# Output stage of a masked triangle product: x added by an accumulating gather for half of the columns, one bias addition on GpSimd

## The chip, the cores and the metric

One core of one Trainium2 chip. The metric is the device time of one execution in microseconds, the median of the runs shown. The engines are TensorE (PE in the profile, its weight loads PEld), VectorE (DVE), ScalarE (ACT), GpSimd (POOL) and SyncE (SP, which only issues transfers); 16 DMA engines move data between the chip's main memory (DRAM) and the on-chip SBUF. Each engine works through its own queue in order and waits on semaphores of the others.

## The reference, cut to what matters

x is 512 x 512 positions of 64 channels, float32. Two layers add to it:

```
x = x + conv0(groupnorm(x))      # layer 0
x = x + spectral(groupnorm(x))   # layer 1: 12 x 12 lowest Fourier modes, mixed over channels

conv0(g):
  n     = layernorm(g)
  left  = (n @ left_w  + left_b ) * mask * sigmoid(n @ lgate_w + lgate_b)
  right = (n @ right_w + right_b) * mask * sigmoid(n @ rgate_w + rgate_b)
  gate  = sigmoid(n @ ogate_w + ogate_b)
  u     = layernorm(einsum('bkjd,bkid->bijd', left, right)) @ out_w + out_b
  return u * gate
```

The part that matters here is the end of layer 0: x1 = x + u * sigmoid(rs * (x' @ W) + ogate_b), where rs is the reciprocal standard deviation of a position.

## The kernel before, in words

The mask has one value per row, and only rows with the mask set take part in the triangle product, so the kernel sorts those rows to the front (`src_i` holds for each rank the row of x) and computes the product for at most 256 rows. The `compact` branch is the one that runs. Its stages: statistics of x (to about 180 us), left and right factors, the triangle product, then the **output stage** that the change touches (first the layer norm and output weights of the product, giving u, then the units described below, about 800 to 1450 us), and a final stage that adds the Fourier part and writes the result (bound by its transfers).

In the output stage a **unit** is 32 columns j of two blocks of 128 rows: 128 partitions x 64 positions x 64 channels, two megabytes. There are 32 units (16 column groups by two halves of the ranks). The half with ranks from 256 on has no masked row: there u is only the row `bias_row_out`. A unit is worked in 8 steps n of 8 positions, and its 64 positions also make four tiles c = 0..3 of 16 positions, `z_t` (128 x 1024 elements, four buffers). Half r = 0 of a unit is c = 0 and 1, half r = 1 is c = 2 and 3.

The order of work is written out by hand: one loop over steps s issues, for every engine, the instructions of step s, and no scheduler moves them. v is the unit, n the step. In one step:

- TensorE: `transpose(s + 13)` (four 128 x 128 transposes of x, L1038; ScalarE copies them out, L1040), `times` with the gate weights into `w_ps` (L1045, two buffers), `times` with the centring matrix for step s + 12 into `c_ps` (L1045, two buffers), and at n = 0 and 4 of the next unit `transform` (L1140), the column Fourier sums of the finished halves r = 0 and r = 1.
- ScalarE: the copy L1040, the sigmoid of one tile at even n (L1221), at n = 5 the square root for the next unit (`root`, L1089, which loads another function table, as the sigmoid after it does again), the square of `c_ps` (L1076), and after every second unit the copy `save` (L1148).
- VectorE: four of the 32 group statistics of the unit before (`statistics`, L1168, from n = 3 on), every second step a reduction of the squares (L1083), the product of `w_ps` and rs (L1274), and at odd n the bias addition of the tile just completed (L1280). Every fourth unit it joins statistics (L1173 to L1186).
- GpSimd: `gated` (L1109), z = z * u, at odd n, and `added` (L1113), x = x + z, at even n, four of each per unit; and two gathers of x (L638, `load`, 1 MB each) for the unit v + 3 at n = 3 and n = 6. Both run on the GpSimd queue; a gather lands in one of five rotating x buffers (`places`).
- SyncE: `store` (L1129) writes a finished half of x1 to DRAM, r = 0 at n = 7 of its unit and r = 1 at n = 3 of the next; `load_u` (L1100) issues 32 small copies of u every second unit.

The order of GpSimd's queue in a unit before, from n = 3: gated(0), gather, added(0), gated(1), added(1), gather, gated(2), then in the next unit's steps 0 to 2 added(2), gated(3), added(3). The last tile of the last unit goes a way of its own (`finished`, on VectorE).

Of the kernel before, what the change touches and what calls it, by code (L numbers as in the profile page):

```python
# [17 lines left out]
P = 128  # L18
N = 512
C = 64  # L20
# [26 lines left out]
def conv_preact_kernel(ctx: ExitStack, tc: tile.TileContext, t: dict):  # L47
# [573 lines left out]
    def compact(fc):  # L621
# [12 lines left out]
            hb[:, :, :M2].rearrange("p b (m k) -> p b m k", k=2), slot_t[:, :, 2:].rearrange("p b (k m) -> p b m k", k=2)  # L634
        )

        def gather(dst, src, idx, r, jc):
            nc.gpsimd.indirect_dma_start(  # L638
                out=dst, out_offset=None, in_=src, in_offset=bass.IndirectOffsetOnAxis(ap=idx[:, r, jc : jc + 1], axis=0)
            )  # L640

        def slots_of(engine, jc, first=0, last=JC):
# [188 lines left out]
        with tc.tile_pool(name="tri", bufs=1) as trp:  # L831
# [92 lines left out]
            with tc.manual_schedule(), tc.tile_pool(name="late", bufs=1) as lp:  # L924
# [65 lines left out]
                with tc.tile_pool(name="np_x", bufs=LEAD + 2) as tp, tc.tile_pool(name="np_q", bufs=2) as sqp, tc.tile_pool(  # L990
# [28 lines left out]
                    def x_of(k):  # L1019
                        return place(order[k % RING])  # L1020
# [67 lines left out]
                        rss[k] = small.tile([P, SIZE * 8], F32, name="rs_n")  # L1088
                        nc.scalar.activation(rss[k], totals[k % 2], AF.Sqrt, bias=eps, scale=1.0 / C)  # L1089

                    def load(k, r):
                        jc, half = units[k]
                        gather(
                            x_of(k)[:, r * JC : (r + 1) * JC].rearrange("p j c -> p (j c)"), tiles, src_i, 2 * half + r, jc
                        )

                    def load_u(jc):
# [4 lines left out]
                    def gated(k, c):  # L1102

                        jc, half = units[k]
                        if half == 0:
                            u = us[jc][:, 16 * (c % 2) : 16 * (c % 2) + 16, c // 2, :]
                        else:
                            u = rows_of["out"].unsqueeze(1).to_broadcast([P, 16, C])
                        nc.gpsimd.tensor_mul(zs[k, c], zs[k, c], u)  # L1109

                    def added(k, c):
                        xr = x_of(k)[:, 16 * c : 16 * c + 16, :]
                        nc.gpsimd.tensor_add(xr, xr, zs.pop((k, c)))  # L1113
# [79 lines left out]
                    for s in range(-LEAD, total_g + 2 * SIZE):  # L1193
# [3 lines left out]
                        def held(i):  # L1197
                            return 0 <= v - i < len(units)
# [13 lines left out]
                            del xts[s]  # L1212
                        if 0 <= s + LEAD - 1 < total_g:
                            cps = centered(s + LEAD - 1)
                        if n in (0, 4) and held(1):
                            transform(v - 1, n // 4)

                        if n % 2 == 0:
                            i, c = (0, n // 2 - 1) if n >= 2 else (1, 3)
                            if held(i):  # L1220
                                nc.scalar.activation(zs[v - i, c], zs[v - i, c], AF.Sigmoid)  # L1221
                        if n == 5 and 0 <= k + 1 < first + len(units):
# [5 lines left out]
                        if n == 3 and held(2) and v % 4 == 1:  # L1228
                            join_squares(v // 4 - 1)

                        if n % 2 == 1:
                            i, c = (0, (n - 3) // 2) if n >= 3 else (1, 3)
                            if held(i) and (v - i, c) != (last, 3):
                                gated(v - i, c)
                            elif held(i):
                                finished()
                        else:
                            i, c = (0, (n - 4) // 2) if n >= 4 else (1, 2 + n // 2)
                            if held(i) and (v - i, c) != (last, 3):
                                added(v - i, c)  # L1240
                        if 0 <= v + 3 < len(units):
                            if n == 3:
                                load(v + 3, 0)
# [20 lines left out]
                        if wps is not None:  # L1264
                            c, odd = divmod(n, 2)
                            if not odd:
                                z = zp.tile([P, 16, C], F32, name="z_t")
                            if k < first:
                                rs = factors[k % 2][:, 16 * c : 16 * c + 16].rearrange("p (h e i) -> p h e i", h=2, e=2)
                                rs = rs[:, :, odd].unsqueeze(3).to_broadcast([P, 2, 4, C])  # L1270
                                nc.vector.tensor_mul(of_pair(z, odd), wps, rs)
                            else:
                                rs = rss[k][:, 8 * n : 8 * n + 8].unsqueeze(2).to_broadcast([P, 8, C])
                                nc.vector.tensor_mul(z[:, 8 * odd : 8 * odd + 8, :], wps, rs)  # L1274
                            if odd:
                                if k < first:
                                    bias = rows_of["out"].unsqueeze(1).to_broadcast([P, 16, C])
                                    nc.gpsimd.tensor_add(z, z, bias)  # L1278
                                else:
                                    nc.vector.tensor_add(z, z, bias_ps["ogate"].unsqueeze(1).to_broadcast([P, 16, C]))  # L1280
                                if k < first:
                                    j = JC * k + 8 * c
                                    nc.sync.dma_start(
                                        u_d[:, j : j + 8].rearrange("p j r c -> p (j r c)"), z.rearrange("p n c -> p (n c)")
                                    )
                                else:
                                    zs[v, c] = z

                        if n == 7 and held(0) and v < last:
                            store(v, 0)  # L1290
                        if n == 3 and held(1) and v - 1 < last:
                            store(v - 1, 1)
                        if n == 6 and v - 1 == last:
# [240 lines left out]
```

## Time and profile before

| | |
|---|---|
| runs shown | 1771.41, 1774.15, 1779.44 us; median 1774.15 |
| profiled execution | 1777.78 us, its span 1776.0 us |
| TensorE, VectorE, ScalarE, GpSimd busy over the span | 88%, 80%, 53%, 53% |
| DRAM read, written | 311.60 MB, 204.60 MB |
| 64 gathers of x in the output stage | GpSimd 983 ns each, landing 6.4 us after issue (median) |
| 127 sums and 127 products on GpSimd (L1113, L1109) | 2372 and 2371 ns each |
| 128 bias sums on VectorE (L1280) | 1221 ns each |
| 128 sigmoids on ScalarE (L1221) | 1058 ns each |

How to read the profile: the page gives busy times of the engines over the span and in 40 slices of 44.4 us. The windows table gives the same for stretches of one's choice. A line of the groups or of the timeline names start and duration in us, engine, code line, operation, out<-in by the program's names, shape, count, and in brackets how long the engine was idle ahead of it and which engine ended that. A DMA line gives the median time from issue to landing.

### The profile page before, as it was taken

How to read it: one execution, taken by the hardware profiler on the slowest of the kernel's cores; microseconds unless marked ns; L12 is line 12 of the kernel's file. 1: busy time of each engine (PE TensorE's matmuls, PEld its weight loads, DVE VectorE, ACT ScalarE, POOL GpSimd, SP SyncE). 2: the span in 40 equal slices, each digit the busy share in tenths (PEclk: the TensorE clock that was granted, in tenths of full speed). 3: DMA queues.
4: the chain of work that ended last, by engine and by line, in shares of the span. 5: the costliest groups of instructions: out<-in, count | busy, mean ns of one | idle time of the engine just before them, and what ended most of it. 6: DMA issues, size and time to landing. Idle time of an engine off the chain costs nothing. (4 is left out here: it accounts for less than half of the span.)

```text
span 1776.0 us, 32619 instructions
## 1 busy us (share of the span) xinstructions
PE 1567.8 (88%) x10918; PEld 1242.0 (70%) x10918; DVE 1413.7 (80%) x2982; ACT 933.0 (53%) x1660; POOL 936.5 (53%) x695
## 2 busy tenths in 40 slices
PE   6779799997999978899999999999999977998772
PEld 5667666662899867787888888888888745665341
DVE  7989678887455568688999999999999984865451
ACT  3666566663333266676777777777777742011000
POOL 4666211111000037698999999999999881111110
PEclk9999999999899999899999999999999976555555
DMA  7999278878898789868767767776776699999999
GB/s 281 386 386 388 107 206 227 229 229 245 279 305 303 257 246 347 298 196 296 265 242 257 253 233 259 264 249 239 249 264 244 212 318 400 425 427 427 426 427 385
DMA packets 192593, 518.48 MB, mean 292 GB/s; under 512 B 37664, under 2 KB 104480, under 8 KB 151456
## 3 DMA queue, kind: packets, MB, share of 16 engines
q1 hardware_dynamic: 156112, 295.65, 47.5%
q0 software_dynamic: 32832, 218.45, 33.4%
q10 hardware_dynamic: 3472, 2.20, 0.5%
q8 instruction: 89, 1.46, 0.3%
q14 instruction: 88, 0.72, 0.1%
HBM read 311.60 MB, written 204.60 MB: 291 GB/s over the span
## 5 line engine op out<-in xcount | busy, mean ns | idle before, releaser
L1045 PE MATMUL w_ps<-gate_x,xt_c 128*128 128x128 f32 x2048 | 280.5, 281 | 30.0 <-DVE z_t L1274 28.6
L1113 POOL TENSOR_TENSOR places<-places,z_t 128x1024 f32<-128x1024 f32 x127 | 301.3, 2372 | 8.0
L1045 PEld LDWEIGHTS w_ps<-gate_x,xt_c 128*128 128x128 f32 x2048 | 252.0, 194 | 46.4 <-DVE z_t L1274 44.6
L1045 PE MATMUL c_ps<-center_x,xt_c 128*128 128x128 f32 x2048 | 277.0, 279 | 0.8 <-ACT xt_c L1040 0.4
L1045 PEld LDWEIGHTS c_ps<-center_x,xt_c 128*128 128x128 f32 x2048 | 252.8, 194 | 3.8 <-ACT xt_c L1040 3.0
L1440 PE MATMUL l_ps<-places,rinv 24*128 24x512 f32 x512 | 206.2, 1118 | 29.3 <-DVE places L1447 19.0
L1168 DVE BATCH_NORM_STATS2 stats2c<-places 128x6 f32<-128x128 f32 x1024 | 220.5, 278 | 9.9 <-POOL places L1113 9.9
L1083 DVE TENSOR_REDUCE scratch<-sq_c 128x16 f32<-128x1024 f32 x160 | 194.6, 1216 | 31.1 <-ACT sq_c L1078 16.1
L1221 ACT ACTIVATE z_t<-z_t 128x1024 f32<-128x1024 f32 x128 | 135.5, 1058 | 131.8 <-DVE z_t L1280 131.1
L1440 PEld LDWEIGHTS l_ps<-places,rinv 24*128 24x128 f32 x512 | 119.8, 302 | 110.8 <-DVE places L1447 56.9
L1278 POOL TENSOR_TENSOR z_t<-z_t,bias_row_out 128x1024 f32<-128x1024 f32 x32 | 75.6, 2363 | 226.3 <-PE y_ps L1058 202.1
L1040 ACT ACTIVATE xt_c<-t_ps,ab_xc 128x512 f32<-128x512 f32 x256 | 176.0, 688 | 11.5 <-PE t_ps L1038 10.6
L1274 DVE TENSOR_TENSOR z_t<-w_ps,rs_n 128x512 f32<-128x512 f32 x256 | 172.0, 672 | 6.2 <-PE w_ps L1045 6.1
L1076 ACT ACTIVATE sq_c<-c_ps 128x512 f32<-128x512 f32 x256 | 150.8, 589 | 31.4 <-PE c_ps L1045 30.8
L1280 DVE TENSOR_TENSOR z_t<-z_t,scratch 128x1024 f32<-128x1024 f32 x128 | 156.3, 1221 | 9.9 <-ACT rs_n L1089 3.7
L688 DVE BATCH_NORM_STATS2 stats1c<-x_ps 128x6 f32<-128x512 f32 x256 | 157.1, 682 | 7.7 <-PE x_ps L687 7.4
L1109 POOL TENSOR_TENSOR z_t<-z_t,places 128x1024 f32<-128x1024 f32 x64 | 151.8, 2371 | 14.6 <-ACT z_t L1221 14.4
L1038 PE MATMUL t_ps<-c_ident,places 128*128 128x128 f32 x1024 | 158.4, 278 | 0.0
L1038 PEld LDWEIGHTS t_ps<-c_ident,places 128*128 128x128 f32 x1024 | 118.5, 142 | 51.4 <-issue 51.4
L1447 DVE TENSOR_TENSOR places<-places,l_ps 128x512 f32<-128x512 f32 x176 | 109.3, 682 | 55.2 <-DMA places<-x_h,dst_i 42.1
L1109 POOL TENSOR_TENSOR z_t<-z_t,bias_row_out 128x1024 f32<-128x1024 f32 x63 | 149.4, 2372 | 5.8 <-ACT z_t L1221 5.5
L673 ACT COPY xc<-xg 128x128 f32 x352 | 105.0, 298 | 66.1 <-POOL xc L673 47.1
(214 smaller groups left out, 2557.0 us busy)
## 6 DMA issues: line engine op xcount, KB each, us to landing
x_h<-places SPq DMA_DIRECT2D x64, 1024.0 KB
out_x<-places SPq DMA_DIRECT2D x44, 1024.0 KB
places<-u_d SPq DMA_DIRECT2D x512, 64.0 KB
out_x<-lx_t SPq DMA_DIRECT2D x20, 1024.0 KB
rbc<-rs_d POOLq DMA_DIRECT2D x32, 512.0 KB, 7.1
left_d<-o_c SPq DMA_DIRECT2D x64, 256.0 KB
right_d<-o_c SPq DMA_DIRECT2D x64, 256.0 KB
left_raw<-left_d SPq DMA_DIRECT2D x64, 256.0 KB
```

The source lines that it names most:

```text
L688: nc.vector.bn_stats(stats[:, 0, 16 * (jc % quarter) + 4 * r + c, :], ps.rearrange("p i k -> p (i k)"))
L1038: nc.tensor.transpose(tps[:, i, :], flat[:, o : o + P], ident)
L1040: nc.scalar.activation(xts[s], tps, AF.Identity, bias=ab1[:, 2:3])
L1045: nc.tensor.matmul(ps[:, 2 * i : 2 * i + 2, :], xts[s][:, i, :], w, start=True, stop=True)
L1076: nc.scalar.activation(sq, cps, AF.Square)
L1083: nc.vector.tensor_reduce(totals[k % 2][:, 8 * (n - 1) : 8 * (n + 1)], sqs.pop(s // 2), AX.X, ALU.add)
L1109: nc.gpsimd.tensor_mul(zs[k, c], zs[k, c], u)
L1113: nc.gpsimd.tensor_add(xr, xr, zs.pop((k, c)))
L1168: nc.vector.bn_stats(st[k // 4][:, g, k % 4, :], x_of(k)[:, :, 2 * g : 2 * g + 2])
L1274: nc.vector.tensor_mul(z[:, 8 * odd : 8 * odd + 8, :], wps, rs)
L1280: nc.vector.tensor_add(z, z, bias_ps["ogate"].unsqueeze(1).to_broadcast([P, 16, C]))
L1440: nc.tensor.matmul(ps.rearrange("p j o -> p (j o)"), rinv[h, b, :], it[h], start=True, stop=True, tile_position=(32 * g, 0),)
```

## The change

For tiles c = 0 and 1 (half r = 0 of a unit) `gated` writes the product over x in the x buffer, and x is added by a second gather of the same megabyte with the operation add, at n = 7; `added` is left for c = 2 and 3. The bias of tile c = 1 is added on GpSimd at n = 4 (`biased`, new), no longer on VectorE. With it, the sigmoids move from n = 0, 2, 4, 6 to 0, 2, 5, 6; the products from n = 1, 3, 5, 7 to 1, 3, 6, 7; the transform of half r = 0 from n = 0 to n = 2 of the next unit; its store from n = 7 to n = 1 of the next unit.

```diff
-        def gather(dst, src, idx, r, jc):
+        def gather(dst, src, idx, r, jc, op=ALU.bypass):
             nc.gpsimd.indirect_dma_start(
-                out=dst, out_offset=None, in_=src, in_offset=bass.IndirectOffsetOnAxis(ap=idx[:, r, jc : jc + 1], axis=0)
+                out=dst, out_offset=None, in_=src, in_offset=bass.IndirectOffsetOnAxis(ap=idx[:, r, jc : jc + 1], axis=0),
+                compute_op=op,
             )
...
-                        nc.gpsimd.tensor_mul(zs[k, c], zs[k, c], u)
+                        if c < 2:
+                            nc.gpsimd.tensor_mul(x_of(k)[:, 16 * c : 16 * c + 16, :], zs.pop((k, c)), u)
+                        else:
+                            nc.gpsimd.tensor_mul(zs[k, c], zs[k, c], u)
+
+                    def biased(k, c):
+                        bias = rows_of["ogate"].unsqueeze(1).to_broadcast([P, 16, C])
+                        nc.gpsimd.tensor_add(zs[k, c], zs[k, c], bias)
...
-                        if n in (0, 4) and held(1):
+                        if n in (2, 4) and held(1):
                             transform(v - 1, n // 4)
 
-                        if n % 2 == 0:
-                            i, c = (0, n // 2 - 1) if n >= 2 else (1, 3)
+                        if n in (0, 2, 5, 6):
+                            i, c = {0: (1, 3), 2: (0, 0), 5: (0, 1), 6: (0, 2)}[n]
                             if held(i):
                                 nc.scalar.activation(zs[v - i, c], zs[v - i, c], AF.Sigmoid)
...
-                        if n % 2 == 1:
-                            i, c = (0, (n - 3) // 2) if n >= 3 else (1, 3)
+                        if n == 7 and held(0):
+                            load(v, 0, ALU.add)
+                        if n in (1, 3, 6, 7):
+                            i, c = {1: (1, 3), 3: (0, 0), 6: (0, 1), 7: (0, 2)}[n]
                             if held(i) and (v - i, c) != (last, 3):
                                 gated(v - i, c)
                             elif held(i):
                                 finished()
-                        else:
-                            i, c = (0, (n - 4) // 2) if n >= 4 else (1, 2 + n // 2)
-                            if held(i) and (v - i, c) != (last, 3):
-                                added(v - i, c)
+                        if n == 4 and held(0):
+                            biased(v, 1)
+                        if n in (0, 2):
+                            c = 2 + n // 2
+                            if held(1) and (v - 1, c) != (last, 3):
+                                added(v - 1, c)
...
-                                else:
+                                elif c != 1:
                                     nc.vector.tensor_add(z, z, bias_ps["ogate"].unsqueeze(1).to_broadcast([P, 16, C]))
...
-                        if n == 7 and held(0) and v < last:
-                            store(v, 0)
+                        if n == 1 and held(1) and v - 1 < last:
+                            store(v - 1, 0)
```

More of the change, by code (lines that the diff above doesn't have):

```diff
@@ L1089, in root, with load @@
                         nc.scalar.activation(rss[k], totals[k % 2], AF.Sqrt, bias=eps, scale=1.0 / C)
-                    def load(k, r):
+                    def load(k, r, op=ALU.bypass):
                         jc, half = units[k]
                         gather(
-                            x_of(k)[:, r * JC : (r + 1) * JC].rearrange("p j c -> p (j c)"), tiles, src_i, 2 * half + r, jc
+                            x_of(k)[:, r * JC : (r + 1) * JC].rearrange("p j c -> p (j c)"), tiles, src_i, 2 * half + r, jc, op
                         )
```

## The prediction, as put on record

> **What bounds the kernel now.** I read the busy tenths by slice first (the output stage is slices 18 to 32, the only ones with PE, DVE and POOL all near 9), then the windows table inside that stage, then the timelines of one unit.
>
> ```profile
> core 0: us, PE busy (x) PEld busy (x) DVE busy (x) ACT busy (x) POOL busy (x), PEclk, DMA share, GB/s
> 860.00:940.00 80.00, 76.75 (x653) 67.92 (x652) 78.86 (x186) 58.89 (x89) 76.95 (x38) 1.00 0.71 254
> ```
>
> VectorE works 78.86 of 80 us, GpSimd 76.95, TensorE 76.75: three engines with almost no room, at a full clock. The DMA engines still have 29% free. GpSimd's timeline of one unit:
>
> ```profile
> 849.53 2.38 POOL L1113 TENSOR_TENSOR places<-places,z_t 128x1024 f32<-128x1024 f32 x1
> 851.85 2.38 POOL L1109 TENSOR_TENSOR z_t<-z_t,bias_row_out 128x1024 f32<-128x1024 f32 x1
> 854.31 2.36 POOL L1113 TENSOR_TENSOR places<-places,z_t 128x1024 f32<-128x1024 f32 x1
> 856.83 0.98 POOL L638 DMA_INDIRECT places<-in_x,src_i  x1
> 857.82 2.40 POOL L1109 TENSOR_TENSOR z_t<-z_t,bias_row_out 128x1024 f32<-128x1024 f32 x1
> ...
> 867.39 2.37 POOL L1109 TENSOR_TENSOR z_t<-z_t,places 128x1024 f32<-128x1024 f32 x1
> 869.90 0.98 POOL L638 DMA_INDIRECT places<-in_x,src_i  x1
> 870.91 2.38 POOL L1113 TENSOR_TENSOR places<-places,z_t 128x1024 f32<-128x1024 f32 x1
> ```
>
> No line carries an idle time: eight products and sums and two gathers fill the unit, 849.53 to 870.91 = 21.38. Start to start: a sum takes 2.32, a product 2.46, either before a gather 2.52, a gather 1.00. Over the stage the first gather of a unit starts at 805.87 and, 26 units later, at 1372.69: **21.80 us a unit**. Three in four take 21.3 to 21.4, set by GpSimd; every fourth 22.4 or more, when VectorE's join of the statistics makes GpSimd wait. So GpSimd binds, and VectorE (1.4% idle) is right behind.
>
> **The change, part by part**, per unit (32 units).
>
> VectorE loses one bias sum: 1.22 (L1280 mean 1221 ns). It then has about 20.3 of work in a unit.
>
> GpSimd loses two sums, gains a bias sum of the same shape (the nearest row, L1278 in the earlier stage, is 2363 ns, so 2.4) and a third gather. The order is now: bias(1), product(1), gather, adding gather, product(2), sum(2), product(3), sum(3), next unit's product(0), gather. Without waits: bias 2.37; product(1) 2.52; two gathers 2.00; 2.46 + 2.32 + 2.46 + 2.32 = 9.56; product(0) and gather 3.52. Sum 19.97, which would be a gain of 1.4.
>
> Two new waits eat it. **First gap:** between bias(1) and product(1) stands ScalarE's sigmoid of the same tile, and GpSimd has nothing queued between them. Sigmoid 1.06 (L1221), plus about 0.09 into ScalarE and 0.08 out of it (880.18 to 880.26 in the trace): 1.23. Loop 21.20.
>
> **Second gap:** ScalarE's order is now sigmoid(1), square root of the next unit with its table load, square, transposed-tile copy, table load, sigmoid(2). Its timeline shows that stretch:
>
> ```profile
> 895.76 1.28 ACT L1089 ACT_TABLE_LOAD   x1
> 897.06 0.31 ACT L1089 ACTIVATE rs_n<-scratch,eps 128x64 f32<-128x64 f32 x1
> 897.27 0.59 ACT L1076 ACTIVATE sq_c<-c_ps 128x512 f32<-128x512 f32 x1
> 897.75 0.59 ACT L1148 COPY places<-f_ps 128x512 f32<-128x512 f32 x1
> 898.21 0.71 ACT L1040 ACTIVATE xt_c<-t_ps,ab_xc 128x512 f32<-128x512 f32 x1
> 898.94 1.28 ACT L1221 ACT_TABLE_LOAD   x1
> 900.24 1.06 ACT L1221 ACTIVATE z_t<-z_t 128x1024 f32<-128x1024 f32 x1
> ```
>
> 895.76 to 901.30 = 5.54 back to back; 5.06 in units without the L1148 copy (every other); mean 5.30, with handoffs 5.40. GpSimd, released by the end of sigmoid(1), is ready for product(2) after 0.08 + 2.52 + 2.00 = 4.60. It waits 0.80. **Loop 22.0 us**, against 21.80: the freed time is given back. This does not hang on the price of issuing the adding gather: no row shows one; below, it is the plain 1.00; above, 1.8 is still hidden in the second gap. What waits behind sigmoid(1) on ScalarE (root, square, tile copy) has slack: VectorE needs the root four steps later.
>
> Before, the fourth units' extra (mean 0.4) came from VectorE, which now has 1.5 of room; I cost it at 0 to 0.2.
>
> **The adding gather's landing** decides the rest. It is issued right behind another 1 MB gather on the same queue, and three things wait for it: TensorE's transform of the first half (now step 2, queued ahead of all later transposes and products), SyncE's store, VectorE's statistics. The store costs nothing: SyncE waited 220.9 us for GpSimd's sums, 31 times, already, and behind the store stand the other stores and the u copies (some 19 us of issue in two units). Gathers reuse a store's buffer ten steps later instead of twelve, still over 25 us. The statistics need sum(3) anyway. The transform is the tight one. TensorE after a transform:
>
> ```profile
> 1023.44 1.06 PE L1140 MATMUL f_ps<-places,hb 128*32 128x512 f32 x8
> 1024.44 0.66 PE L1038 MATMUL t_ps<-c_ident,places 128*128 128x128 f32 x4
> ...
> 1028.94 0.60 PE L1038 MATMUL t_ps<-c_ident,places 128*128 128x128 f32 x4
> ```
>
> ScalarE cannot reach sigmoid(1), at step 5, before it has evicted the third of these transposes. So from the landing: transform 1.00, two full steps 4.50, transpose 0.60, tile copy 0.70, then sigmoid and handoffs 1.24, product(1) 2.52, gather 1.00, and the next adding gather is issued: 11.6. The loop is landing time L + 11.6, and L may be up to 10.4 before it exceeds 22.0.
>
> L: the second gathers of seven units landed 5.4 to 12.4 us after issue, median 7.0.
>
> ```profile
> places<-in_x,src_i POOLq DMA_INDIRECT x64, 6.4
> ```
>
> (The last column is the median of all such gathers.) The adding gather comes 1.0 behind, so 6.0 remain, and then its own transfer. A plain gather keeps the 16 engines 3.0 us each (27.7% of 480 us over 44 gathers). An addition must read the destination too. Below: like a plain gather, L = 6.0 + 3.0 = 9.0. Above: three times, for read, read and write one after another, L = 15. I take the read of x as a gather and the second megabyte at the 427 GB/s of the last stage's slices, 2.46: **L = 11.5**, loop 23.1. That is nearest to the rows, since only bytes are added. The load fits: 0.72 x 21.8 = 15.7 busy, plus 5.5, is 21.2 of 23.1.
>
> On this the Trainium skill (DMA: Bandwidth & Descriptors) says, in the rules for kernel authors, that an accumulating DMA reads its destination and writes it later; no run here shows it yet, and it speaks against a transfer at a plain gather's price. The same page's fit in its section on one DMA of the gpsimd path, 2.0 us and bytes over 436e3, gives 4.4 for a megabyte, an estimate; the quickest row here is 5.4, so the fit is a floor. With its 2.4 for each megabyte L would be 10.8 and the sum below 19 us instead of 42.
>
> **The sum.** 23.1 - 21.8 = 1.3, by 32 units = 42 us. Nothing outside the stage changes: the final stage is bound by its transfers (DMA share 1.00 after 1500 us) and merely starts later. The profiled execution took 1777.78 (span 1776.0), the median of three 1774.15; I add to the median: **1816 us**. Own range, from L = 10.6 to 12.9: 1787 to 1860.
>
> **Rivals.**
> A. *The landing is hidden.* At L = 9.0 the loop is GpSimd's and ScalarE's 22.0 plus up to 0.2, and some units with a late gather ahead: +6 to +20, 1778 to 1795, say 1785. For it: 29% free DMA time. Against: half of the measured second gathers took over 7.0.
> B. *Faster.* GpSimd is the limit and loses work; if the second gap does not open, the loop is 21.20, -0.6 by 32 = -19: 1755. It decides from the point where ScalarE's stretch from sigmoid(1) to the end of sigmoid(2) falls under 4.9 (then the loop is under 21.5 and the kernel over 0.5% faster), and L stays under 10. For it: the stage has three full engines and two are relieved. Against: the two table loads and the four activations are rows, and the order on ScalarE is fixed.
> C. *Additions are slow.* L = 15 gives a loop of 26.6, +154: 1928; from L = 13 on, over 1862. For it: nothing in the trace shows an addition's rate. Against: only 1 MB each.
>
> **How the numbers follow.** Forecast 0.47, A 0.25, B 0.15, C 0.13. The range leaves out C and small tails: 1754 to 1862. A difference below 0.5% (8.9 us) cannot be told from none. Faster by more: B, 0.15. Within: nearly half of A, 0.12. Slower: the rest, 0.73.
>
> **What would show it.** In the changed profile the bias sum on GpSimd must be followed by about 1.2 idle put down to ScalarE's sigmoid, and product(2) by a wait of 0.3 to 1.1 or none if the issue of the adding gather takes over 1.0. TensorE must wait for a transfer ahead of the first transform; if it does not, A holds. The landing of the third gather must read 10.6 to 13. VectorE's busy share in the stage must fall to about 20.3 in a period of 23. If GpSimd stays without gaps, my order of waits is wrong and B holds; if the gathers land after 14 us, C.

## The result, and the profile after

The changed kernel takes **1908.57 us** (median of four runs, 1902.68 to 1911.43), the kernel before 1776.8 in the runs beside it: 1.074 times as long, with a 95% interval of 1.070 to 1.078. The profiled execution took 1911.43, its span 1909.6, which is 133.6 above the span before. I had forecast slower, but 1816 and at most 1862.

First the windows table of the changed kernel, for the stretch that the prediction quoted of before:

```profile
core 0: us, PE busy (x) PEld busy (x) DVE busy (x) ACT busy (x) POOL busy (x), PEclk, DMA share, GB/s
860.00:940.00 80.00, 65.62 (x527) 57.11 (x525) 61.15 (x147) 48.82 (x74) 59.33 (x31) 0.94 0.84 253
```

Three engines had 77 to 79 of 80 us to do before. Now no engine is near its limit: TensorE 65.62, VectorE 61.15, GpSimd 59.33. Only the DMA share has risen, from 0.71 to 0.84, and the granted clock, 1.00 before, is 0.94. Where every engine idles, a wait that goes round in a circle is the first thing to look for. GpSimd's timeline shows one turn of it, and it is a long one:

```profile
1005.19 2.36 POOL L1111 TENSOR_TENSOR places<-z_t,places 128x1024 f32<-128x1024 f32 x1 [3.27 <-ACT z_t L1229]
1007.70 0.97 POOL L638 DMA_INDIRECT places<-in_x,src_i  x1 [0.16 <-issue]
1008.98 1.58 POOL L638 DMA_INDIRECT places<-in_x,src_i  x1 [0.30 <-issue]
1010.25 2.71 POOL L1113 TENSOR_TENSOR z_t<-z_t,places 128x1024 f32<-128x1024 f32 x1
...
1022.60 1.00 POOL L638 DMA_INDIRECT places<-in_x,src_i  x1
1029.26 2.37 POOL L1117 TENSOR_TENSOR z_t<-z_t,bias_row_ogate 128x1024 f32<-128x1024 f32 x1 [5.65 <-DVE z_t L1286]
1035.15 2.36 POOL L1111 TENSOR_TENSOR places<-z_t,bias_row_out 128x1024 f32<-128x1024 f32 x1 [3.52 <-ACT z_t L1229]
1037.66 0.96 POOL L638 DMA_INDIRECT places<-in_x,src_i  x1 [0.15 <-issue]
1038.92 1.58 POOL L638 DMA_INDIRECT places<-in_x,src_i  x1 [0.30 <-issue]
1040.70 2.37 POOL L1113 TENSOR_TENSOR z_t<-z_t,bias_row_out 128x1024 f32<-128x1024 f32 x1 [0.20 <-ACT z_t L1229]
```

The second of each pair of gathers is the adding one (L1121 is now x = x + z, L1111 and L1113 the products, L1117 GpSimd's bias). From one adding gather to the next this unit takes 1038.92 - 1008.98 = 29.94 us. The bias stands 5.65 for VectorE, which itself had nothing to work on: in the trace the adding gather of 1008.98 landed 14.6 us after its issue, at 1023.6, and TensorE's timeline shows who stood for it:

```profile
1023.76 1.94 PE L1148 MATMUL f_ps<-places,hb 128*32 128x512 f32 x8 [5.63 <-DMA places<-in_x,src_i]
1025.62 1.12 PE L1039 MATMUL t_ps<-c_ident,places 128*128 128x128 f32 x4
1026.53 1.92 PE L1046 MATMUL w_ps<-gate_x,xt_c 128*128 128x128 f32 x8
1028.24 1.35 PE L1046 MATMUL c_ps<-center_x,xt_c 128*128 128x128 f32 x8
1029.43 0.60 PE L1039 MATMUL t_ps<-c_ident,places 128*128 128x128 f32 x4
...
1031.74 1.06 PE L1148 MATMUL f_ps<-places,hb 128*32 128x512 f32 x8
1032.74 0.66 PE L1039 MATMUL t_ps<-c_ident,places 128*128 128x128 f32 x4
```

Two things are to be seen. Ahead of the third transpose after the landing (1032.74) stand two transforms, not one. And after the stall of 5.63 us the first four groups take 1.94, 1.12, 1.92 and 1.35 us; the same groups, a few microseconds on, take 1.06, 0.66, 1.06 and 1.06. In a unit where TensorE waited 1.09 only, the same instruction is at once as short as ever:

```profile
1074.06 1.06 PE L1148 MATMUL f_ps<-places,hb 128*32 128x512 f32 x8 [1.09 <-DMA places<-in_x,src_i]
1075.06 0.66 PE L1039 MATMUL t_ps<-c_ident,places 128*128 128x128 f32 x4
```

The windows of the 5 us from each of these two starts tell them apart by the granted clock, 0.50 and 1.00:

```profile
1023.76:1028.76 5.00, 5.00 (x23) 3.34 (x24) 1.13 (x5) 0.69 (x1) 0.00 (x0) 0.50 0.88 213
1074.06:1079.06 5.00, 5.00 (x44) 4.16 (x45) 4.58 (x12) 2.38 (x5) 4.80 (x4) 1.00 0.87 367
```

The table of waits between 860 and 1400 us (us in total, times, longest) has the circle's members:

```profile
ACT xt_c L1041 <- PE t_ps L1039: 86.8, 41, 8.6
PE f_ps L1148 <- DMA places<-in_x,src_i: 64.3, 20, 7.7
POOL places L1111 <- ACT z_t L1229: 48.8, 15, 3.9
DVE z_t L1292 <- ACT rs_n L1090: 35.2, 21, 1.7
```

The landing holds TensorE, TensorE's transpose holds ScalarE, ScalarE's sigmoid holds GpSimd's product, and behind that product the next adding gather is issued. The page's chain of the work that ended last, of which DMA had 9% before, agrees:

```profile
DMA 34%; PE 26%; POOL 6%; issue 5%; SPq 3%; ACT 1%; DVE 1%; ACTq 0%; POOLq 0%; DVEq 0%
```

Last, the queues between 860 and 1340 us (packets, MB, share of the 16 engines; q0 carries GpSimd's gathers), of before:

```profile
q1 hardware_dynamic: 66124, 73.61, 43.6%
q0 software_dynamic: 6335, 46.13, 27.7%
```

and of the changed kernel:

```profile
q0 software_dynamic: 7980, 58.17, 44.6%
q1 hardware_dynamic: 54734, 63.16, 38.9%
```

With a unit of 25.7 us the stretch holds 18.7 units: 0.446 x 480 / 18.7 = 11.5 us of each engine for a unit's three gathers. If the two copying ones take 3.0 each, as before, the adding one takes 5.5 for one megabyte. That is an estimate: the same working gives 4.6 to 5.3 in `e3_first`, `e4_late`, `e5_bias_back`, `e7_all` and `e16_back_late`.

### The profile page after: what moved, and what is told of

Same layout as the page of the kernel before. It is cut to its first block, busy times and chain, and to the rows that moved or that the text cites. A ratio compares the mean times of both kernels' runs of the same rounds, so it can differ in the third digit from the quotient of the medians.

```text
span 1909.6 us, 32489 instructions
## 1 busy us (share of the span) xinstructions
PE 1584.2 (83%) x10918; PEld 1258.5 (66%) x10918; DVE 1380.7 (72%) x2950; ACT 936.9 (49%) x1660; POOL 911.8 (48%) x695
## 4 chain that ended last, share of the span: by engine, by line
DMA 34%; PE 26%; POOL 6%; issue 5%; SPq 3%; ACT 1%; DVE 1%; ACTq 0%; POOLq 0%; DVEq 0%
DMA places<-in_x,src_i 14%; DMA out_x<-places 6%; PE tri_c_ps L896 6%; PE l_ps L1452 4%; PE w_ps L1046 3%; PE c_ps L1046 3%; DMA places<-tri_d 3%; PE side_ps L874 3%; DMA places<-u_d 2%; PE t_ps L1039 2%; DMA out_x<-lx_t 2%; DMA x_h<-places 2%; PE f_ps L1148 2%; PE y_ps L1059 2%; POOL places L638 2%
## 5 line engine op out<-in xcount | busy, mean ns | idle before, releaser
L1046 PE MATMUL w_ps<-gate_x,xt_c 128*128 128x128 f32 x2048 | 290.1, 287 | 32.4 <-DVE z_t L1286 32.3
L1046 PEld LDWEIGHTS w_ps<-gate_x,xt_c 128*128 128x128 f32 x2048 | 262.7, 201 | 49.9 <-DVE z_t L1286 46.5
L1176 DVE BATCH_NORM_STATS2 stats2c<-places 128x6 f32<-128x128 f32 x1024 | 220.6, 278 | 31.1 <-DMA places<-in_x,src_i 23.3
L1290 POOL TENSOR_TENSOR z_t<-z_t,bias_row_out 128x1024 f32<-128x1024 f32 x32 | 75.5, 2363 | 225.6 <-PE y_ps L1059 201.2
L1148 PE MATMUL f_ps<-places,hb 128*32 128x512 f32 x512 | 76.4, 671 | 107.1 <-DMA places<-in_x,src_i 107.1
L1039 PE MATMUL t_ps<-c_ident,places 128*128 128x128 f32 x1024 | 164.1, 285 | 0.0
L1292 DVE TENSOR_TENSOR z_t<-z_t,scratch 128x1024 f32<-128x1024 f32 x96 | 117.2, 1221 | 62.9 <-ACT rs_n L1090 60.7
L1121 POOL TENSOR_TENSOR places<-places,z_t 128x1024 f32<-128x1024 f32 x63 | 148.9, 2363 | 4.9
L638 POOL DMA_INDIRECT places<-in_x,src_i x96 | 113.4, 1181 | 27.9 <-issue 11.6
```

The costliest lines, as they stand in the source:

```text
L638: nc.gpsimd.indirect_dma_start(out=dst, out_offset=None, in_=src, in_offset=bass.IndirectOffsetOnAxis(ap=idx[:, r, jc : jc + 1], axis=0), ...
L1039: nc.tensor.transpose(tps[:, i, :], flat[:, o : o + P], ident)
L1046: nc.tensor.matmul(ps[:, 2 * i : 2 * i + 2, :], xts[s][:, i, :], w, start=True, stop=True)
L1176: nc.vector.bn_stats(st[k // 4][:, g, k % 4, :], x_of(k)[:, :, 2 * g : 2 * g + 2])
```

## The experiments

Theory one: the landing loop. The unit is the time from issue to landing of the adding gather, plus a fixed way from there to the next one (TensorE, ScalarE, GpSimd). Against it stand two rivals: what the change moves between GpSimd, ScalarE and VectorE holds the unit, whatever the transfer does; and the load that the addition puts on the DMA engines holds it, wherever its landing is awaited. The expectations state what each gives in their run. Ratios are to the kernel before, with 95% intervals. "Unit" is the mean period in the profiled execution, "landing" the median time from the issue of the third gather of a unit to its landing, over those whose landing the trace tells.

**Is it the addition?** `e1_plain` copies instead of adding, which leaves the product out of half of the output; `e2_none` has no third gather, which leaves x out of that half. The diff is that of the first.

```diff
-                            load(v, 0, ALU.add)
+                            load(v, 0)
```

> The second gather of a half copies instead of adding, everything else as in the changed kernel (the product of that half is overwritten by x, so that half of the output is left without it). Theory 1 (the landing of the adding gather ahead of TensorE's first transform sets the loop; an addition costs about twice a copy): the landing falls from 12.1 to 8 to 9.5 us, loop of landing + 12.9 us about 21.5, so the 22.0 us of GpSimd and ScalarE bind: 1775 to 1800 us. Theory 2 (the new waits between GpSimd and ScalarE make the time, whatever the gather costs): stays at 1890 to 1910 us.

> The adding gather is left out, everything else as in the changed kernel (x is not added in half of the columns). Theory 1: nothing waits for a landing; the loop of GpSimd and ScalarE remains, 21.2 to 22.0 us a unit: 1755 to 1785 us, and GpSimd shows its gap of about 1.2 us ahead of the second product. Theory 2: 1880 us or more.

Measured: with a copy 1834.43, 1.031 (1.029 to 1.034), unit 23.2, landing 8.4; without a gather 1796.11, 1.009 (1.007 to 1.011), unit 22.45. So of the 132 us, 17 to 19 are there without any third gather, some 38 come with a copy, and another 74 with the addition. Both expectations were too low. With the first 17 to 19 come the gaps on GpSimd, which the prediction had priced at 6 in all (a loop of 22.0 against 21.80); its timeline without the gather:

```profile
1012.49 2.39 POOL L1117 TENSOR_TENSOR z_t<-z_t,bias_row_ogate 128x1024 f32<-128x1024 f32 x1
1016.04 2.35 POOL L1111 TENSOR_TENSOR places<-z_t,places 128x1024 f32<-128x1024 f32 x1 [1.17 <-ACT z_t L1229]
1018.54 0.98 POOL L638 DMA_INDIRECT places<-in_x,src_i  x1 [0.15 <-issue]
1021.10 2.36 POOL L1113 TENSOR_TENSOR z_t<-z_t,places 128x1024 f32<-128x1024 f32 x1 [1.58 <-ACT z_t L1229]
```

1.17 behind the bias, and 1.58 ahead of product(2), where no second gather fills the gap. Between 860 and 1340 us the waits for these sigmoids are 33.1 us in 22 times ahead of L1111 and 41.6 in 24 ahead of L1113, so the unit shown has rather short ones. What the 38 us of the copy consist of, no run singled out.

**Is it the landing?** `e3_first` issues the adding gather ahead of the plain one, so that no megabyte goes in front of it; `e4_late` puts both transforms at step 4, two steps later for the first. The first two pieces of the diff are the one, the last is the other.

```diff
-                        if n == 7 and held(0):
-                            load(v, 0, ALU.add)
...
+                        if n == 6 and held(0):
+                            load(v, 0, ALU.add)
...
-                        if n in (2, 4) and held(1):
-                            transform(v - 1, n // 4)
+                        if n == 4 and held(1):
+                            transform(v - 1, 0)
+                            transform(v - 1, 1)
```

> The adding gather is issued ahead of the plain gather of step 6 instead of behind it. Theory 1: the issue comes 1.3 us earlier and nothing stands ahead of it on its queue. If its 12.1 us are to a good part the transfer ahead (3 us of engine time), the landing falls to about 9 us and the loop to about 20.6, below the 22.0 of GpSimd and ScalarE: 1775 to 1800 us. If the addition alone takes its 11 us, the loop is 11 + 11.6 = 22.6 us: about 1805 us. Theory 2: no change, 1890 to 1910 us.

> TensorE's transform of the first half is moved from step 2 to step 4, right ahead of that of the second half. Theory 1: the landing may come two steps (4.4 us of TensorE work) later; what still waits for it is VectorE's statistics at step 3, with a loop of landing + about 9.1 us = 21.2: 22.0 us bind, in units with a late landing (14 to 17 us) some more: 1780 to 1815 us. Rival (VectorE's statistics or the load on the DMA engines, 0.85 busy, set the loop): 1860 us or more.

Measured: 1863.79, 1.046 (1.043 to 1.049), unit 24.3, landing 9.6 in place of 11.2; and 1851.35, 1.041 (1.039 to 1.044), unit 23.7, landing 11.8. Each lies between its two expectations and gives back some 45 to 57 us, so the landing loop is real: in `e4_late` TensorE's wait for the landing has fallen to 1.4 us in all, 2 times, between 860 and 1340 us, from 58.4, 18 times, in the changed kernel. Neither comes near the time before: something else holds the unit at 23.7 once the landing has 4.5 us more slack. So far theory one accounts for less than half of the loss.

**One half of the change at a time.** `e5_bias_back` keeps the accumulation and returns the bias of tile 1 to VectorE; `e12_bias_only` puts only that bias on GpSimd into the kernel before. The diff is that of the first, whose products go back to n = 1, 3, 5, 7 as well.

```diff
-                        if n in (0, 2, 5, 6):
-                            i, c = {0: (1, 3), 2: (0, 0), 5: (0, 1), 6: (0, 2)}[n]
+                        if n in (0, 2, 4, 6):
+                            i, c = {0: (1, 3), 2: (0, 0), 4: (0, 1), 6: (0, 2)}[n]
...
-                        if n == 4 and held(0):
-                            biased(v, 1)
...
-                                elif c != 1:
+                                else:
```

> The bias of the second tile is back on VectorE, its sigmoid and product on steps 4 and 5 as before; the adding gather and all else as in the changed kernel. If the loop is the landing plus what stands between it and the next adding gather, that stretch loses the bias sum on GpSimd and one step of TensorE: landing 12 + about 10 = 22 us a unit, VectorE needs 21.5: 1780 to 1815 us. If the DMA engines' work (6.4 us of 16 engines for an addition) or the landing alone sets the time, 1870 us or more.

> The other part alone: the kernel before, with the bias of the second tile on GpSimd and its sigmoid and product on steps 5 and 6, and no adding gather; four products, four sums and a bias sum on GpSimd. GpSimd's own work is 21.34 + 2.39 = 23.7 us a unit, +1.9 by 32 = +62: 1830 to 1850 us, VectorE idle for over 2 us a unit. If VectorE had been the limit: 1760 us or less.

Measured: 1843.47, 1.034 (1.030 to 1.039), unit 23.7, between the two expectations; and 1831.96, 1.029 (1.026 to 1.032), as expected: nine sums and products and two gathers were put at 23.7 us, and GpSimd is busy for 78 of 80 us in the windows between 940 and 1340. Either half alone is a loss, and in the first the DMA share of the 80 us windows stands at 0.85 to 0.95.

**All remedies together.** `e6_none_swap` has no adding gather and fills the gap behind the bias: the bias goes ahead of the product of tile 0, which fills the time of the sigmoid. `e7_all` is the whole computation with that swap, the gather in front and the late transforms; `e8_all_plain` the same with a copy. The diff shows the swap alone.

```diff
-                        if n in (1, 3, 6, 7):
-                            i, c = {1: (1, 3), 3: (0, 0), 6: (0, 1), 7: (0, 2)}[n]
+                        if n == 4 and held(0):
+                            biased(v, 1)
+                        if n in (1, 4, 6, 7):
+                            i, c = {1: (1, 3), 4: (0, 0), 6: (0, 1), 7: (0, 2)}[n]
...
-                        if n == 4 and held(0):
-                            biased(v, 1)
...
-                            if n == 3:
+                            if n == 4:
                                 load(v + 3, 0)
```

> No adding gather (x is not added in half of the columns), and on GpSimd the bias sum stands ahead of the first product instead of behind it, with the gather of step 3 behind both, so that a product and a gather lie between the bias sum and the product that needs its sigmoid. If the 22.45 us a unit without the gather came from GpSimd's two gaps, they close: VectorE's 20.4 and GpSimd's 19 to 20 us are left, 20.5 to 21.3 a unit: 1735 to 1762 us. If something else held it (ScalarE, TensorE), 1785 to 1800 us.

> Adding gather ahead of the plain one, both transforms at step 4, and the bias sum ahead of the first product on GpSimd. If only waits made the change slow, they are gone and GpSimd's 20.8 us a unit bind: 1745 to 1765 us. If the DMA engines are the next limit (15.7 us of work a unit before, 6.4 more for the addition, is 22.1 us), 22.3 to 23.2 us a unit: 1790 to 1820 us with a DMA share over 0.95.

> The same with a copying instead of an adding gather (the product of half of the columns is overwritten by x and left out). DMA work 15.7 + 3 = 18.7 us a unit. If DMA work limits the version with the addition, this one falls to GpSimd's 20.5 to 21.3 us: 1735 to 1765 us. If it stays within 10 us of the version with the addition, a wait that the reordering left is the limit.

Measured: 1786.74, 1.004 (1.003 to 1.006); 1838.63, 1.034 (1.032 to 1.036), unit 23.3; 1817.54, 1.023 (1.020 to 1.027), unit 22.9. The swap won 9 of the 17 to 19 us and no more, and with every remedy the whole computation still loses 60, more than either of its expectations allowed; a copy in place of the addition gives 21 of them back. One window of `e7_all`:

```profile
1020.00:1100.00 80.00, 74.41 (x612) 65.93 (x613) 65.98 (x164) 51.20 (x76) 69.11 (x35) 0.96 0.90 280
```

No engine is full and the DMA share is 0.90.

**ScalarE's square root.** In the waits VectorE's bias sum (L1292) now stands for `rs_n` (L1090). Both read the PSUM tile `scratch`, and the root comes behind sigmoid(1) on ScalarE, hence behind GpSimd's bias. First I gave VectorE's sum a row in SBUF, which takes the shared tile away: `e9_none_sbuf` (on `e6_none_swap`), `e10_sbuf` (on the changed kernel), `e11_all_sbuf` (on `e7_all`).

```diff
-                                    nc.vector.tensor_add(z, z, bias_ps["ogate"].unsqueeze(1).to_broadcast([P, 16, C]))
+                                    nc.vector.tensor_add(z, z, rows_of["ogate"].unsqueeze(1).to_broadcast([P, 16, C]))
```

> No adding gather, the bias sum ahead of the first product on GpSimd (as in the run that gave 1786.7 us), and VectorE's three bias sums read the bias row from SBUF instead of the PSUM tile that ScalarE's square root reads too (x is not added in half of the columns). If VectorE's wait for the root (34.5 us in 23 units, 1.5 us a unit) is what gave the relief of VectorE back, it goes, and 20.6 to 21.3 us a unit remain: 1740 to 1765 us. If another wait takes its place, 1778 us or more.

> The changed kernel with VectorE's bias sums reading from SBUF, nothing else. If the landing of the adding gather sets the loop, VectorE's wait for the root lies beside it: 1890 to 1912 us. If the wait for the root is a good part of the loss (1.5 us by 32 units), 1850 to 1870 us.

> Adding gather first, both transforms at step 4, bias sum ahead of the first product, and VectorE's bias from SBUF: the full computation with every wait found so far taken away. If the DMA engines' 21 to 22 us of work a unit are the floor, 22 to 22.8 us a unit: 1785 to 1810 us, not faster than before. If waits were all, GpSimd's 20.8: 1745 to 1765 us.

Measured: 1835.43, 1.031 (1.028 to 1.034); 1925.59, 1.082 (1.076 to 1.088); 1873.93, 1.054 (1.051 to 1.057): all three slower than their originals, the second by less than the intervals tell apart. The wait for the root went, and a worse one came. The timeline of `e9_none_sbuf`, VectorE and GpSimd side by side:

```profile
1051.41 2.36 POOL L1113 TENSOR_TENSOR z_t<-z_t,bias_row_out 128x1024 f32<-128x1024 f32 x1 [1.06 <-ACT z_t L1229]
...
1051.55 3.30 DVE L1290 TENSOR_TENSOR z_t<-z_t,bias_row_ogate 128x1024 f32<-128x1024 f32 x1
...
1053.84 3.23 POOL L1121 TENSOR_TENSOR places<-places,z_t 128x1024 f32<-128x1024 f32 x1
```

The sum that started while GpSimd's product ran took 3.30, that is until 1.1 after the product's end; GpSimd's sum, begun in its turn while VectorE's ran, took 3.23. Means in the stage are 2206 ns for VectorE's sum (L1290) and 3233 for GpSimd's (L1121), against 1221 and 2363 in the changed kernel. The Trainium skill (SBUF — State Buffer, "SBUF: two separate sides") says that a VectorE operation with two SBUF operands and a GpSimd operation that reads SBUF exclude each other for a whole instruction, and these two rows agree. The experiment had changed two things, so it says nothing on the root.

The second try moves the root ahead of sigmoid(1) on ScalarE and leaves the operand in PSUM: `e13_none_root` (on `e6_none_swap`), `e14_all_root` (on `e7_all`), `e15_all_root_plain` (on `e8_all_plain`).

```diff
+                        if n == 5 and 0 <= k + 1 < first + len(units):
+                            root(k + 1)
                         if n in (0, 2, 5, 6):
...
-                        if n == 5 and 0 <= k + 1 < first + len(units):
-                            root(k + 1)
```

> No adding gather, bias sum ahead of the first product on GpSimd, and on ScalarE at step 5 the square root ahead of the sigmoid instead of behind it (x is not added in half of the columns). If VectorE's wait for the root (1.5 us a unit) gave its relief back, it goes without any contention: 20.6 to 21.3 us a unit, 1740 to 1765 us. If TensorE or ScalarE hold the unit near 22 us, 1778 us or more.

> The full computation: adding gather first, both transforms at step 4, bias sum ahead of the first product, root ahead of the sigmoid. If the DMA engines' 21 to 22 us of work a unit are the floor: 1790 to 1815 us with a DMA share over 0.93, and GpSimd or VectorE wait for transfers. If only waits on engines were left: 1745 to 1770 us.

> The same with a copying gather (the product of half of the columns is left out of the output). DMA work about 18.7 us a unit. If DMA work limits the version with the addition, this one is 25 us or more faster than it: 1745 to 1775 us. If within 10 us, the addition's price is not what limits it.

Measured: 1787.25, 1.004 (1.002 to 1.006); 1842.83, 1.037 (1.031 to 1.042); 1821.85, 1.024 (1.021 to 1.027). No change against the originals. VectorE's wait for the root fell from 31.0 us in `e6_none_swap` to 11.4 and the time stayed, so that wait is not what holds the unit: that theory fell. The waits of `e13_none_root` between 860 and 1340 us show what took its place:

```profile
POOL places L1111 <- ACT z_t L1231: 25.5, 18, 2.2
...
DVE scratch L1084 <- ACT sq_c L1077: 17.0, 21, 0.9
...
PE c_ps L1046 <- ACT xt_c L1041: 14.3, 19, 1.0
```

ScalarE now loads two function tables with only the root between them (1.28 each in its timeline), and in that time TensorE waits for its tile copy and VectorE for its square, in place of the root.

**Biases back, and the landing far away.** Last, three runs with all biases on VectorE, so that neither the gap behind GpSimd's bias nor the root plays a part: `e17_back_none` without the adding gather, `e16_back_late` with it and both transforms at step 4, `e18_back_late_first` with it issued in front as well. Their edits are those shown above, put together.

> All four biases on VectorE, the products of the first half written over x, no adding gather at all (x is missing from that half). GpSimd has six tensor operations and two gathers, about 16.7 us, and VectorE its 21.5 us of before. If the bias on GpSimd and the root behind it were what held the units in the runs without a gather (1787 to 1796), this one is VectorE's: unit 21.5 to 21.9, 1765 to 1780. If the place of the products alone costs, it stays at 1785 or more.

> All four biases on VectorE, the adding gather kept, both transforms at step 4 (full computation). In the run with the biases back and the transform at step 2, TensorE waited 30.4 us in 20 units for the landing, 1.5 us a unit, and the unit was 23.68. If that wait is what the gather costs there, the unit falls to 22.2 and the time to 1785 to 1800. If the gather costs by the load it puts on the DMA engines, or by what it delays on GpSimd's queue, the wait appears elsewhere and the time stays above 1820.

> As the run with late transforms and the biases back, but with the adding gather issued ahead of the plain one (full computation). Its landing was 1.6 us shorter in that order (9.6 against 11.2). If the landing still gates, this run is 20 to 50 us below the other; if it doesn't, both are equal within 10 us. Beating the time before (1777) would need a unit under 21.8.

Measured: 1781.36, 0.999 (0.997 to 1.000), against 1783.28 before; 1857.16, 1.042 (1.040 to 1.044); 1854.4, 1.039 (1.036 to 1.042).

Without the gather, writing the product over x costs nothing. It gains nothing either, though GpSimd has lost two of its eight sums and products. The windows of `e17_back_none`:

```profile
940.00:1020.00 80.00, 76.46 (x645) 69.22 (x644) 77.59 (x184) 58.53 (x87) 57.65 (x29) 0.98 0.76 260
1200.00:1280.00 80.00, 76.59 (x658) 68.30 (x657) 78.20 (x185) 59.98 (x89) 56.86 (x30) 1.00 0.72 243
```

GpSimd has fallen from 76.95 to between 56 and 61 in the windows from 940 to 1340, VectorE stays at 78 and is the one engine left without room (TensorE 76.5). The unit is theirs, and relieving GpSimd does not shorten it.

With the gather some 75 us come back although its landing is awaited two steps later, and issuing it in front changes nothing, which speaks against the landing here; in `e16_back_late` TensorE's first transform waits for it 6.1 us in all, 3 times. The waits of `e16_back_late`, first SyncE's queue, then GpSimd's gathers, between 860 and 1340 us:

```profile
SPq L1101 <- DMA places<-u_d: 110.1, 46, 5.0
```

```profile
POOL places L638 <- DVE stats2c L1176: 17.0, 4, 7.7
POOL places L638 <- PE t_ps L1039: 11.8, 6, 3.6
POOL places L638 <- PE c_ps L1046: 10.4, 5, 9.0
```

SyncE's line was 5.2 us, 10 times, before, and 8.0, 10 times, in `e17_back_none`. SyncE's timeline shows what it does to the order; of before:

```profile
894.15 18.97 SPq L1100 DMA_DIRECT2D places<-u_d  x32
913.22 3.05 SPq L1162 DMA_DIRECT2D modes_d<-places  x4
916.38 16.57 SPq L1129 DMA_DIRECT2D x_h<-places  x4
```

and of `e16_back_late`:

```profile
968.10 29.99 SPq L1101 DMA_DIRECT2D places<-u_d  x32
999.52 1.69 SPq L1170 DMA_DIRECT2D modes_d<-places  x4
1003.38 3.55 SPq L1137 DMA_DIRECT2D x_h<-places  x4
```

The 32 small copies of u take 30 us to issue instead of 19, because each waits for an earlier one (SyncE's transfers take eight semaphores in turn, so that each waits for the eighth before it); the four stores of two units stand behind them and go out in one burst. GpSimd's next gather, ready at 1003.85, starts at 1011.51. The profile names VectorE's statistics and TensorE as releasers, whoever ended last; but by the order of work the statistics of that buffer were done at step 2, and what was still open was a store. The trace's semaphores settle it: this gather waits for the semaphore of the first of the four stores (issued 1003.38), which landed at 1010.72, 0.79 us ahead of the gather's start. The same holds, at 0.76 to 1.12 us, for 14 waits of gathers between 860 and 1340 us, 49.2 us in all; in `e18_back_late_first` they are 79.0, in `e17_back_none` and in the changed kernel none. The backlog also outlasts the stage: from GpSimd's last sum to the end of the span it is 345.1 us in this run, 331.3 in the changed kernel and 323.6 before.

The queues suggest the reason for the backlog, though no run shows it by itself. In `e16_back_late` a unit takes 23.1 us and its transfers 20.9 us of each of the 16 engines (0.466 + 0.438 of 480 us over 20.7 units), a share of 0.90; at the 21.8 us of before it would be 0.96. The highest share that a window of this stage shows, in any run, is 0.95, in `e5_bias_back`; the runs with the addition and late transforms, `e11_all_sbuf` aside, stand at 0.85 to 0.94. No version of the change that adds by a gather came under a unit of 23.1, and none beat the kernel before.

## Why the prediction was right on the sign and wrong on the size

**Right.** That the freed work on GpSimd is eaten by two gaps (1.17 and 1.58 in the unit of `e2_none` shown, against 1.23 and 0.80 priced, the second larger there because no gather stands in it). That the issue of the adding gather, 1.58 against 0.98, stays hidden in the second gap: 0.20 is left of it in the long unit above. That TensorE's transform is the place where the landing is awaited. The price of the adding gather, 5.5 of each engine by the estimate above. The landing itself: 11.5 predicted, 11.2 median and 12.0 mean measured.

**The step that failed** is "the loop is landing time L + 11.6". From the landing to the next adding gather the trace has 12.9 in thirteen units (one of them: issue 1062.95, landing 11.0 later, next issue 1086.83) and 14.4 to 15.3 in eleven in which TensorE was slow behind the landing (the long one shown: 1023.6 to 1038.92); one unit near the start took 19.4. Three things were missing:

- The second half's transform at step 4 also stands between the landing and the third transpose (1079.65 and 1031.74 in the trace): 1.00. I counted "two full steps" and forgot that one of them has a transform in it.
- Two gathers back to back start 1.27 apart, not 1.00: each adding gather has 0.30 of waiting ahead of it.
- TensorE restarts slowly. Of the 28 waits of a first transform for the landing between 780 and 1520 us nine were of 3.7 us or more, and behind each of them groups ran at about half speed, as in the window above with the granted clock 0.50; of the eight of up to 2.05 us none was followed by slow groups; of the eleven between, 2.1 to 3.1 us, five were. At all fourteen slow restarts, and at none of the others, the trace's record of the granted clock reads 0.50, for 3.4 or 6.8 us. They cost 1.4 to 2.4 us each, 23 in all. The Trainium skill (TensorE: Matmul & The Clock Gate, Part 1) describes half the clock after an idle window of about 3.4 us, full clock after as long a busy one, and a window that runs free of what the kernel does. The half clock, the 3.4 us and a loss of about half as much agree; that five waits shorter than it were followed by slow groups does not follow from the page, and there the trace decides.

The sum then runs: 1.3 more in the loop by 32 units, 42 us; the mean landing 12.0 for 11.5, 16; the restarts 23; and a longer way from the stage to the end, 331.3 for 323.6, 8. With the 42 forecast these are 131 of the 133.6 measured; the rest is not assigned. This says what sets the unit in the changed kernel, not what it would be worth to take the landing away: the next limit lies close, at 23.7 in `e4_late`.

**Not seen at all** were two waits that lie beside the landing in the changed kernel. VectorE's relief is taken back: its bias sum (L1292) waited 3.7 us for ScalarE's root on the page of before and 60.7 now, more than the 39 us (32 by 1.22) that it was spared. I had written that the root "has slack", because VectorE needs its value four steps later. The code takes its reciprocal two steps later, at n = 7, and VectorE's sum reads the same PSUM tile at n = 5. The wait is real, but `e13_none_root` took most of it away and won nothing, so it is not shown as a cost. And I costed the later store at nothing, since SyncE was waiting anyway. In the changed kernel no gather waits for a store; with the copies of u slowed and the landing out of the way it is SyncE that is late, and the gathers with it (`e16_back_late`).

**The rivals.** A (landing hidden) falls: TensorE waits for the transfer in 20 of 21 units. B (faster) did not have its condition: the second gap is there (1.58 in `e2_none`). Nor does less work on GpSimd help where the gaps are gone or changed: without gather and without GpSimd's bias (`e17_back_none`) the time is that of before, VectorE being full, and with the bias moved and put in front (`e6_none_swap`) it is 1.004. C (slow addition, L = 15) gave nearly the measured time, 1928, but for a wrong reason: the mean landing is 12.0, and L = 15 is passed in 3 of the 29 units whose landing the trace tells.

**Open.** What holds the unit at 22.3 without a gather (`e6_none_swap`, `e13_none_root`) and at 22.9 with a copying one (`e8_all_plain`, `e15_all_root_plain`) when no engine has over 76.2 of 80 us of work in a window: waits between TensorE, ScalarE, VectorE and GpSimd take each other's place there, and no run singled one out.

## What to carry to other kernels

When a transfer is put into a loop, write the way from its landing to its next issue instruction by instruction, with everything queued on each engine on that way, and add the stall's own price on TensorE; the constant matters as much as the landing. Where two engines are full, taking work off one showed nothing here (1.00 without the gather), and giving it to the other or to the DMA engines has to be paid from their slack: with 29% free DMA time no arrangement tried here could carry one more megabyte with an addition without loss. A cost that is hidden today (the store behind the copies of u) is to be priced for the case that its cover goes.

## What the runs showed of the hardware

- An adding gather of 1 MB takes about 5 us of each DMA engine (estimates of 4.6 to 5.5) against 3.0 for a copying one, and 1.58 us of GpSimd to issue against 0.98. Two gathers issued back to back start 1.27 us apart.
- A VectorE sum of two SBUF operands beside GpSimd's work takes 2.2 us instead of 1.22 with one operand in PSUM, and GpSimd's own sum takes 3.23 instead of 2.36 (means of `e9_none_sbuf` and the changed kernel).
- Behind each of nine waits of 3.7 us or more TensorE's granted clock was 0.50 for 3.4 or 6.8 us, behind none of eight waits of up to 2.05 us, and behind five of eleven between; a slow restart cost 1.4 to 2.4 us.
- SyncE took 30 us instead of 19 to issue the same 32 copies, each waiting for the eighth before it, when the DMA share was 0.9 instead of 0.7 (`e16_back_late` and before).
